# A mixture-of-experts block on one core: attention scores by column quarters of TensorE, turned by VectorE, and router logits by differences

## The chip, the core and the metric

The kernel runs on one core of a Trainium2 chip. TensorE (PE) multiplies 128x128 tiles, VectorE (DVE) and ScalarE (ACT) do elementwise work, GpSimd (POOL) does some of it too, and SyncE (SP) mostly issues transfers; each runs its own instructions in order and waits on semaphores. The metric is the device time of one execution in microseconds; before the change it is 472.56 us, the median of three runs (471.83 to 472.63).

## What is computed

All data are fp32. For 8 sequences of 512 tokens of width 256 (`x`), each with 64 context rows and an anchor vector:

```python
nx = layer_norm(x, gamma, beta)
scores = einsum('bth,bph->btp', nx @ Wq, ctx @ Wk) * 256 ** -0.5
weights = softmax(scores)
evidence = einsum('btp,bph->bth', weights, ctx @ Wv)
combined = concat([nx, evidence, anchor])                  # width 768
router_probs = softmax(combined @ router_W + router_b)     # 3 experts
h = silu(einsum('btc,ecr->bter', combined, e_w1) + e_b1)   # 3 x 512
routed = sum_e((h_e @ e_w2_e + e_b2_e) * router_probs_e)
g = sigmoid(silu(combined @ gate_w1 + gate_b1) @ gate_w2 + gate_b2)
out = x + g * (routed @ out_w + out_b)
```

Neither softmax changes when one number is taken from all the scores (or logits) of a token; the change rests on that.

## The kernel before

The eight sequences ("rows" b0, b1 of a pair) are worked in four pairs, j = 0 to 3. Most tensors are kept transposed, features on partitions and the 512 tokens of a sequence along the free dimension (`nxT`, `h`, `wT`). Products of a 2x2 block form, with the two sequences of a pair as one of the block indices, use seven products for eight (`nx_product` with numbers 1 to 7, sums of x from `combine_x`, sums of weights from `combine`).

**Setup.** Weights are loaded by SP; Wq and Wk are joined with the context into `mr` (`keep_m`), so that scores come straight from `nxT`. x of pair 0 is normalized (`statistics`, `deviation`, `normalize`) and transposed by TensorE (`transpose_x`), scores and softmax follow, then the weights `w` of pair 0 are transposed by four TensorE transposes (`transpose_w`, L583, called in `gate_layer` between products 5 and 2) and copied by ACT. Context values times first-layer weights are `vw` (`value_weights`). `anchor_rows` multiplies the anchors with 32 columns of the array at a time, into four quarters of the partitions.

**Scores** (`scores(b)`, L537): x is stationary (128 features x 128 tokens), `mr` moves, 64 context columns and 3 router columns, so tokens come out on partitions. 8 matmuls for a sequence, two of these calls for a pair. VectorE takes the maximum, ACT does four exps with sums. `router_logits(b)` multiplies the softmax weights with the three router rows of `vw` and sums, on VectorE, in two pieces, and adds the x part (from the score matmul) and the anchor's (`rbias`).

**A pair**: `gate_layer`, three `expert_layer`s, then `outputs`. The first three accumulate x parts and evidence parts (`evidence`, 64-row products) in PSUM; `keep_part` copies a bank by ACT, `add` adds one on VectorE; a product that goes on in a bank waits for the copy or addition that reads it. `weigh` multiplies hidden values by router probabilities on VectorE. `outputs` runs seven expert products per output block, and between them the next pair's scores, softmax, logits and probabilities.

**The order is written out by hand** and kept by the scheduler. Engines run their parts in program order. `put(within, (e, point), step)` places a step at a point of expert e (A after product 5 of the first chunk, B before products 7, C after them, D after products 3), "gate" before product 7 of the gate, "gate end" after its addition; `put(between, point, step)` at a point of `outputs`, whose order is begin, gate, P1, P5, P6, P2, P7, P3, P4. Buffers come from pools by tag: a tile with `bufs=1` reuses the buffer of the one before with that tag, and its writer waits until all readers of the old one are done. Transfers issued by SP or ACT share eight semaphores in program order: each waits until the eighth one before it has landed.

For pairs 1 to 3 the weights `w` go to DRAM and come back in 32x32 blocks (`regroup_w`, one store and four loads at P2), and VectorE turns the blocks (`transpose_w_blocks`). x of later pairs goes the same way (`store_x`, `regroup_x`, `transpose_blocks`).

Of the kernel before, what the change touches and what calls it, by code (L numbers as in the profile page):

```python
# [16 lines left out]
def kernel(  # L17
# [49 lines left out]

    nc = tc.nc
# [11 lines left out]
    SC = CT + E  # L80
# [41 lines left out]
    x_sb = {}  # L122

    def load_x(b):
        x_sb[b] = xpool.tile([P, NT, H], F32, tag="x", name=f"x_{b}")
        nc.sync.dma_start(x_sb[b], x[b].rearrange("(t p) d -> p t d", p=P))
# [24 lines left out]
    rrow = scr[:E, HK : HK + B]  # L151
# [3 lines left out]
    zeros, rows, cond_sb = scr[:, :P], scr[:, P : 2 * P], scr[:B, 2 * P : 2 * P + H]  # L155
    nc.vector.memset(zeros, 0.0)
# [19 lines left out]
    rw = const.tile([P, 3 * KH, E], F32, tag="rw", name="rw")  # L176
    nc.gpsimd.dma_start(rw, rows_of(router_W))
    rb_c = const.tile([E, 1], F32, tag="rb_c", name="rb_c")
    nc.gpsimd.dma_start(rb_c, router_b.rearrange("(e o) -> e o", o=1))
# [4 lines left out]
    w1 = const.tile([P, 2 * KH, R0 + E], F32, tag="w1", name="w1")  # L184
# [51 lines left out]

    mr = const.tile([P, KH, B, SC], F32, tag="mr", name="mr")
    nc.gpsimd.tensor_copy(w1[:, KH:, R0:], rw[:, KH : 2 * KH, :])
    for m in range(KH):
        nc.gpsimd.tensor_copy(mr[:, m, :, CT:], rw[:, m, :].unsqueeze(1).to_broadcast([P, B, E]))  # L240
# [15 lines left out]

    def small_transposes():
        pt = either("pt_rows")
        nc.tensor.transpose(pt[:, :NR], rows, ident[:NR, :NR])
        nc.vector.tensor_copy(cols, pt[:, :NR])  # L260
        nc.gpsimd.tensor_copy(b2T[:, :, :E], b2_c.rearrange("p e k -> p k e"))
        pt = either("pt_cond")
        for k in range(KH):
            nc.tensor.transpose(
                pt[:, k * B : (k + 1) * B], cond_sb[:, k * P : (k + 1) * P], ident[:B, :B]
            )
        nc.vector.tensor_copy(
            condT[:, :, :B], pt[:, : KH * B].rearrange("p (k b) -> p k b", b=B)
        )
# [48 lines left out]
    def keep_m(m, ps):  # L318
        nc.vector.tensor_copy(mr[:, m, :, :CT], ps.rearrange("p (b c) -> p b c", c=CT))
# [3 lines left out]
    rbias = const.tile([P, E, B], F32, tag="rbias", name="rbias")  # L323

    def router_anchor():
        ps = misc("ps_rb")
        for k in range(KH):
            nc.tensor.matmul(
                ps[:E, :B], rw[:, 2 * KH + k, :], condT[:, k, :B], start=(k == 0), stop=(k == KH - 1)
            )  # L330
        nc.vector.tensor_scalar(rrow, ps[:E, :B], rb_c, None, ALU.add)
        rbd = dram.tile([E, B], F32, tag="rbd", name="rbd")
        nc.gpsimd.dma_start(rbd, rrow)
        nc.gpsimd.dma_start(rbias, rbd.partition_broadcast(P))

    def spread_router_rows(j):
        vrd = dram.tile([E, 2 * CT], F32, tag="vrd", name=f"vrd_{j}")
        nc.gpsimd.dma_start(vrd.rearrange("e c -> c e"), S["vw", j][:, R0:])  # L338
        S["vr", j] = work.tile([P, E, 2, CT], F32, tag="vr", name=f"vr_{j}", bufs=1)
        nc.gpsimd.dma_start(  # L340
            S["vr", j].rearrange("p e i c -> p e (i c)"), vrd.partition_broadcast(P)
        )
# [40 lines left out]
    TB = 32  # L383
# [97 lines left out]
    def scale_x(b, k, src, vector):  # L481
        if vector:
            nc.vector.tensor_scalar(
                S["nxT", b][:, k, :], src, gamma_c[:, k : k + 1], beta_c[:, k : k + 1], ALU.mult, ALU.add
            )
        else:
            nc.scalar.activation(
                S["nxT", b][:, k, :], src, AF.Identity, bias=beta_c[:, k : k + 1],
                scale=gamma_c[:, k : k + 1],
            )  # L490

    def transpose_x(b):
        xn = S.pop(("xn", b))
        S["nxT", b] = npool.tile([P, KH, T], F32, tag="nxT", name=f"nxT_{b}")
        for k in range(KH):
# [3 lines left out]
            scale_x(b, k, pt, k % 2 == 0)  # L499

    def store_x(b):
        S["xd", b] = dram.tile([T, H], F32, tag="xd", name=f"xd_{b}")
        nc.sync.dma_start(S["xd", b].rearrange("(t p) d -> p t d", p=P), S.pop(("xn", b)))

    def regroup_x(b):
        xg = work.tile([P, KH, T], F32, tag="xg", name=f"xg_{b}", bufs=1)
        load_blocks(xg, S.pop(("xd", b)))
        S["xg", b] = xg

    def transpose_blocks(b):  # L510
# [3 lines left out]
        for k in range(KH):  # L514
            nc.vector.transpose(nxT[:, k, :], xg[:, k, :])
            scale_x(b, k, nxT[:, k, :], False)
# [12 lines left out]
    def scores(b):  # L529
        nxT, j, i = S["nxT", b], b // 2, b % 2  # L530
        if i == 0:
            S["w", j] = work.tile([P, NT, 2, CT], F32, tag="w", name=f"w_{j}", bufs=1)
        w = S["w", j][:, :, i, :]
        ps = misc(f"ps_s_{b}")[:, : NT * SC].rearrange("p (t c) -> p t c", c=SC)
        for t in range(NT):
            for k in range(KH):
                nc.tensor.matmul(  # L537
                    ps[:, t, :],
                    nxT[:, k, t * P : (t + 1) * P],
                    mr[:, k, b, :],  # L540
                    start=(k == 0),
                    stop=(k == KH - 1),
                )
        mx = work.tile([P, NT], F32, tag="mx", name=f"mx_{b}")
        nc.vector.tensor_reduce(mx, ps[:, :, :CT], AX.X, ALU.max)
        nmx = work.tile([P, NT], F32, tag="nmx", name=f"nmx_{b}")
        nc.vector.tensor_scalar_mul(nmx, mx, -SCALE)
        lg = work.tile([P, NT, E], F32, tag="lg", name=f"lg_{b}")
        nc.vector.tensor_copy(lg, ps[:, :, CT:])
        sm = work.tile([P, NT], F32, tag="sm", name=f"sm_{b}")  # L550
        for t in range(NT):
            nc.scalar.activation(
                w[:, t, :], ps[:, t, :CT], AF.Exp, bias=nmx[:, t : t + 1], scale=SCALE,
                accum_out=sm[:, t : t + 1],
            )
        S["lg", b], S["sm", b] = lg, sm

    def softmax(b):
        w, sm = S["w", b // 2][:, :, b % 2, :], S.pop(("sm", b))
        rs = work.tile([P, NT], F32, tag="rs", name=f"rs_{b}")  # L560
        nc.vector.reciprocal(rs, sm)
        nc.vector.tensor_tensor(w, w, rs.unsqueeze(2).to_broadcast([P, NT, CT]), ALU.mult)

    def regroup_w(j):

        wd = dram.tile([T, P], F32, tag="wd", name=f"wd_{j}")
        nc.sync.dma_start(
            wd.rearrange("(t p) c -> p t c", p=P), S["w", j].rearrange("p t i c -> p t (i c)")
        )
        S["wg", j] = work.tile([P, 1, T], F32, tag="wg", name=f"wg_{j}", bufs=1)  # L570
        load_blocks(S["wg", j], wd)

    def transpose_w_blocks(j):
        S["wT", j] = work.tile([P, T], F32, tag="wT", name=f"wT_{j}", bufs=1)
        nc.vector.transpose(S["wT", j], S.pop(("wg", j))[:, 0, :])

    def transpose_w(j):

        w = S["w", j]
        wT = work.tile([P, T], F32, tag="wT", name=f"wT_{j}", bufs=1)  # L580
        pt = misc(f"pt_w_{j}")
        for t in range(NT):
            nc.tensor.transpose(  # L583
                pt[:, t * P : (t + 1) * P], w[:, t, :, :].rearrange("p i c -> p (i c)"), ident
            )
        nc.scalar.copy(wT, pt)
        S["wT", j] = wT

    def router_logits(b):
        j, i = b // 2, b % 2  # L590
        w, lg, vr = S["w", j][:, :, i, :], S["lg", b], S["vr", j][:, :, i, :]
        le = work.tile([P, NT, E], F32, tag="le", name=f"le_{b}")
        pv = work.tile([P, NT // 2, E, CT], F32, tag="pv", name=f"pv_{b}", bufs=1)
        for t in range(0, NT, NT // 2):
# [653 lines left out]
```

## Time and profile before

| | |
|---|---|
| median of 3 runs | 472.56 us (471.83 to 472.63) |
| profiled execution | 472.56 us; its span from the first to the last instruction 470.4 us |
| PE busy | 465.1 us, 1439 instructions |
| DVE busy | 353.8 us, 653 instructions |
| ACT busy | 215.4 us, 388 instructions |
| POOL busy | 85.1 us, 111 instructions |
| granted TensorE clock, mean | 1.000 |
| score matmuls (L537) | 128 records, two for each fp32 matmul |

The profile's busy rows give an engine's busy time and its share of the span. Its slices cut the span into 40 equal parts, and each digit is the busy share in tenths (PEclk: the granted clock). The chain follows the work that ended last back through whatever released each step. Timeline rows have a start, a length, the engine, the line, the operation, output and inputs, the shape, and in brackets the engine's idle time before the row and who ended it. The rows of transfers give a size and the time from issue to landing. A pair's period, from the first gate product of one `outputs` to the next (`ps_gu`), is 107.55 us.

### The profile page before, as it was taken

To read this page: it belongs to the slowest core of one execution; us is meant where nothing else is said; L and a number is where in the kernel's file an instruction comes from. 1 tells how busy PE (TensorE), PEld (TensorE's weight loads), DVE (VectorE), ACT (ScalarE), POOL (GpSimd) and SP (SyncE) were. 2 spreads that over 40 slices of the span, in tenths; PEclk is the share of its full clock that TensorE was granted. 3 is DMA by queue.
4 is the path that set the end of the run, shared out by engine and by line. 5 is a ranking of instruction groups with operands and counts; after the bars stand their busy time and mean duration, and the time that the engine had idled before them with its cause. 6 is when DMAs were issued, how large, how long until landed. Compare 5 with 4: busy or idle time off the path is not lost.

```text
span 470.4 us, 4664 instructions
## 1 busy us (share of the span) xinstructions
PE 465.1 (99%) x1439; PEld 221.1 (47%) x1439; DVE 353.8 (75%) x653; ACT 215.4 (46%) x388; POOL 85.1 (18%) x111
## 2 busy tenths in 40 slices
PE   9999999999999999999999999999999999999996
PEld 7744546445444444445454444445454444444454
DVE  3755847989989555889989555898989624797972
ACT  3455565657211647657311546658311465457000
POOL 5318123200062300000062300000052400000020
PEclk9999999999999999999999999999999999999999
DMA  9968330056232830442122740352122560000013
GB/s 288 376 108 179 57 136 0 0 117 90 36 67 32 171 135 0 91 88 45 17 47 44 162 152 1 75 106 45 18 45 45 84 186 0 1 0 1 0 22 68
DMA packets 126424, 36.84 MB, mean 78 GB/s; under 512 B 111548, under 2 KB 123392, under 8 KB 125888
## 3 DMA queue, kind: packets, MB, share of 16 engines
q1 hardware_dynamic: 122656, 28.59, 29.1%
q0 software_dynamic: 1856, 7.18, 4.8%
q10 hardware_dynamic: 1888, 0.79, 0.6%
q8 instruction: 11, 0.18, 0.2%
q14 instruction: 13, 0.11, 0.1%
HBM read 28.36 MB, written 8.18 MB: 78 GB/s over the span
## 4 chain that ended last, share of the span: by engine, by line
PE 91%; DVE 4%; SPq 3%; DMA 0%; issue 0%; ACT 0%; ACTq 0%
PE ps_u L677 40%; PE ps_z L677 17%; PE ps_y L677 14%; PE ps_vw L652 4%; SPq L392 3%; PE ps_gu L677 3%; PE ps_s L537 3%; PE ps_w2o L418 2%; PE ps_gz L677 1%; DVE h L951 1%; PE ps_wake L255 1%; DVE h L760 1%; PE ps_m L299 1%; PE ps_v L299 1%; PE ps_gy L677 1%; DVE r L960 0%
## 5 line engine op out<-in xcount | busy, mean ns | idle before, releaser
L760 DVE TENSOR_TENSOR h<-h,pb 128x512 f32<-128x512 f32 x96 | 61.9, 693 | 10.5 <-ACT h L710 10.5
L677 PE MATMUL ps_u<-h,w2o 128*128 128x512 f32 x144 | 63.9, 593 | 0.0
L677 PE MATMUL ps_u<-nxT,w 128*128 128x512 f32 x112 | 55.6, 607 | 0.0
L710 ACT ACTIVATE h<-h,abias 128x512 f32<-128x512 f32 x72 | 49.2, 718 | 8.8 <-DVE h L716 8.2
L677 PE MATMUL ps_z<-wT,vw 64*128 64x512 f32 x104 | 49.5, 605 | 0.0
L983 POOL TENSOR_TENSOR yb<-yb,xb 128x512 f32<-128x512 f32 x14 | 19.1, 1368 | 150.1 <-DVE yb L982 144.7
L677 PE MATMUL ps_z<-h,w2s 128*128 128x512 f32 x96 | 42.8, 595 | 0.2 <-DVE r L966 0.2
L719 ACT COPY h<-ps_u 128x512 f32<-128x512 f32 x48 | 27.9, 582 | 32.2 <-PE ps_u L677 31.9
L677 PEld LDWEIGHTS ps_u<-h,w2o 128*128 128x128 f32 x144 | 27.1, 190 | 31.3 <-issue 29.4
L716 DVE TENSOR_TENSOR h<-h,ps_y 128x512 f32<-128x512 f32 x24 | 16.4, 683 | 28.9 <-PE ps_y L677 25.0
L951 DVE TENSOR_TENSOR h<-h,h 128x1024 f32<-128x1024 f32 x24 | 34.3, 1483 | 0.0
L677 PEld LDWEIGHTS ps_u<-nxT,w 128*128 128x128 f32 x112 | 19.9, 189 | 29.8 <-issue 24.9
L710 ACT ACTIVATE h<-ps_u,abias 128x512 f32<-128x512 f32 x24 | 16.5, 687 | 30.2 <-PE ps_z L677 30.2
L677 PE MATMUL ps_y<-nxT,w 128*128 128x512 f32 x56 | 28.6, 592 | 0.0
L677 PE MATMUL ps_z<-T,ws 128*128 128x512 f32 x56 | 28.6, 592 | 0.0
L677 PEld LDWEIGHTS ps_z<-h,w2s 128*128 128x128 f32 x96 | 17.9, 190 | 22.1 <-issue 21.1
L677 PE MATMUL ps_u<-wT,vw 64*128 64x512 f32 x56 | 27.8, 611 | 0.0
L338 POOL DMA_DIRECT2D vrd<-vw x4 | 3.2, 802 | 132.5 <-ACT vw L659 132.5
L677 PE MATMUL ps_y<-wT,vw 64*128 64x512 f32 x56 | 27.0, 596 | 0.0
L652 PE MATMUL ps_vw<-w,vT 128*128 128x512 f32 (+1 forms) x64 | 26.9, 541 | 0.0
L677 PE MATMUL ps_u<-T,ws 128*128 128x512 f32 x56 | 26.7, 594 | 0.0
L677 PE MATMUL ps_z<-nxT,ws 128*128 128x512 f32 x56 | 26.6, 592 | 0.0
(209 smaller groups left out, 790.2 us busy)
## 6 DMA issues: line engine op xcount, KB each, us to landing
pb<-pd POOLq DMA_DIRECT2D x4, 1536.0 KB, 7.7
x<-in_x_dram SPq DMA_DIRECT2D x8, 512.0 KB, 5.4
xb<-in_x_dram SPq DMA_DIRECT2D x64, 64.0 KB, 2.4
out_dram<-yb SPq DMA_DIRECT2D x56, 64.0 KB, 2.0
w<-in_L_xcond_e_w_dram SPq DMA_DIRECT2D x6, 512.0 KB, 9.5
xd<-x SPq DMA_DIRECT2D x6, 512.0 KB, 2.9
xg<-xd SPq DMA_DIRECT2D x48, 64.0 KB, 2.4
scr_wa<-in_L_xcond_e_w_dram SPq DMA_DIRECT2D x3, 512.0 KB, 10.2
```

The source lines that it names most:

```text
L299: nc.tensor.matmul(ps, w_sb[:, k, m * P : (m + 1) * P], src[:, k, :], start=(k == 0), stop=(k == KH - 1))
L392: nc.sync.dma_start(dst[i * TB : (i + 1) * TB, k, :].rearrange("r (j c) -> r j c", c=TB), src[:, lo : lo + TB].rearrange("(j r) c -> r j c ...
L418: nc.tensor.matmul(ps[:, d * H : (d + 1) * H], w2T[:, k, (i + d) * P : (i + d + 1) * P], ow_sb[:, k, :], start=(k == 0), stop=(k == KH - 1),)
L537: nc.tensor.matmul(ps[:, t, :], nxT[:, k, t * P : (t + 1) * P], mr[:, k, b, :], start=(k == 0), stop=(k == KH - 1),)
L652: nc.tensor.matmul(ps, vT[:, k, j * 2 * CT : (j + 1) * 2 * CT], w1[:, KH + k, n0:n1], start=(k == 0), stop=(k == KH - 1),)
L677: nc.tensor.matmul(ps, lhsT, rhs, start=start, stop=True, skip_group_check=not start)
L710: nc.scalar.activation(h, h if src is None else src, AF.Silu, bias=abias[:, c, 2 * j + i : 2 * j + i + 1])
L716: nc.vector.tensor_tensor(h, h, part, ALU.add)
L719: nc.scalar.copy(chunk(n, i, d), part)
L760: nc.vector.tensor_tensor(h, h, S["pb", j][:, i, 2 * q // RC, :], ALU.mult)
L951: nc.vector.tensor_tensor(d, p, m, ALU.subtract)
L983: nc.gpsimd.tensor_tensor(yb, yb, S["xb", 2 * j + row][:, i, :], ALU.add)
```

## The change

**Scores** are computed once for a pair. The context is stationary, 32 columns of it at a time; x moves, 256 tokens at a time. For row i and half h of the tokens the result goes to partitions 32(2i+h) and up, so four neighbouring matmuls use four column quarters. One VectorE transpose of 32x32 blocks brings tokens to partitions and context to the free dimension. A partition then holds one token of each of 8 blocks, so exps are eight for a pair, 128x64 each, as before.

**Router by differences.** Only logits 1 and 2 minus logit 0 are formed (ED = 2). Context row 0's column is taken from the other columns of `mr` (`keep_m`), so the score of context row 0 is 0 and its column is free: it carries difference 1's x part. Difference 2's x part is a VectorE multiply with a sum along x (`router_part`, four instructions of 128x256 for a sequence) against `gg`, gamma times the weight difference; the beta part goes into `rbias` by two more small matmuls. The context part uses two multiplies of 128x512 and two sums for a pair (`router_logits(j)`).

**Turning the weights** (`turn_weights`): VectorE transposes blocks into `tw`, and transfers from SBUF to SBUF move 32x256 pieces into `wT`: eight on SP's queue for later pairs, four on ACT's queue for pair 0 (there a second VectorE transpose writes the other four in place). This replaces the four TensorE transposes and the ACT copy of pair 0 and the way through DRAM of later pairs. `tw`, `junk` of `router_part` and `pv` of `router_logits` share one buffer (tag "tw").

**Layout.** `load_x` and `store_x` are four transfers of 32 partitions each instead of one of 128; `load_x` and `transpose_x` put the tokens in the order that the quarters need; the probabilities' buffer `pb` has a dimension for the half. SP issues 293 transfers (242 before), ACT 10 (6), POOL 52 (40).

**Places.** For pair 0, both `router_part` calls stand at "gate". A new point W lies between the fourth and fifth `weigh` of an expert. The rest is in the diff, cut to its core:

```diff
 def load_x(b):
-        nc.sync.dma_start(x_sb[b], x[b].rearrange("(t p) d -> p t d", p=P))
+        j, a = b // 2, b % 2
+        for i, h in SIDES:
+            nc.sync.dma_start(x_sb[b][side(i, h), :, :], tile_rows(x[2 * j + i], a, h))
...
 def keep_m(m, ps):
-        nc.vector.tensor_copy(mr[:, m, :, :CT], ps.rearrange("p (b c) -> p b c", c=CT))
+        ps = ps.rearrange("p (b c) -> p b c", c=CT)
+        nc.vector.tensor_copy(m0, ps[:, :, 0])
+        nc.vector.tensor_tensor(
+            mr[:, m, :, 1:], ps[:, :, 1:], m0.unsqueeze(2).to_broadcast([P, B, CT - 1]), ALU.subtract
+        )
...
+    def router_part(b):
+        j, a = b // 2, b % 2
+        lg = logits(j)
+        junk = work.tile([P, H], F32, tag="tw", name=f"junk_{b}", bufs=1)
+        for t in range(NT):
+            nc.vector.scalar_tensor_tensor(
+                junk, S["xn", b][:, t, :], 1.0, gg, ALU.mult, ALU.mult,
+                accum_out=lg[:, 2, a * NT + t : a * NT + t + 1],
+            )
...
+    def scores(j):
+        ps = misc(f"ps_s_{j}")
+        for g in range(2):
             for k in range(KH):
+                for i, h in SIDES:
+                    nc.tensor.matmul(
+                        ps[side(i, h), g * NH : (g + 1) * NH],
+                        mr[:, k, 2 * j + i, g * TB : (g + 1) * TB],
+                        S["nxT", 2 * j + i][:, k, h * NH : (h + 1) * NH],
+                        start=(k == 0),
+                        stop=(k == KH - 1),
+                    )
+        w = work.tile([P, 2, NJ, TB], F32, tag="w", name=f"w_{j}", bufs=1)
+        S["w", j] = w
+        nc.vector.transpose(w.rearrange("p g j c -> p (g j c)"), ps)
+        nc.vector.tensor_copy(logits(j)[:, 1, :], w[:, 0, :, 0])
+        nc.vector.memset(w[:, 0, :, 0], 0.0)
...
+    def turn_weights(j, queue, twice=False):
+        tw = work.tile([P, 2, NH], F32, tag="tw", name=f"tw_{j}", bufs=1)
+        nc.vector.transpose(
+            tw.rearrange("p g t -> p (g t)"), S["w", j].rearrange("p g j c -> p (g j c)")
+        )
         wT = work.tile([P, T], F32, tag="wT", name=f"wT_{j}", bufs=1)
...
+        if twice:
+            nc.vector.transpose(wT, S["w", j].rearrange("p g j c -> p (g j c)"))
+        for i, h in SIDES:
+            for g in range(2):
+                if not twice or g != h:
+                    queue.dma_start(wT[side(i, g), h * NH : (h + 1) * NH], tw[side(i, h), g, :])
...
+    def router_logits(j):
+        w, lg, vr = S["w", j], S["lg", j], S["vr", j]
+        le = work.tile([P, ED, NJ], F32, tag="le", name=f"le_{j}")
+        for e in range(ED):
+            pv = work.tile([P, 2, NJ, TB], F32, tag="tw", name=f"pv_{j}_{e}", bufs=1)
...
         if j == 0:
-            transpose_w(0)
+            turn_weights(0, nc.scalar, twice=True)
...
         if e > 1 or e and j:
-            weigh(j, 5)
+            weigh(j, 4)
+            run("W")
+            weigh(j, 1)
...
+                put(within, "gate", router_part, 0)
+                put(within, "gate", router_part, 1)
                 put(within, "gate", value_weights, 0, 1)
...
-                put(within, (0, "B"), router_logits, 1)
...
-                put(within, (0, "C") if j else (1, "A"), statistics, b1, 0, NT)
+                put(within, (0, "B") if j else (1, "A"), statistics, b1, 0, NT)
                 for i in range(2):
-                    put(within, (1, "C"), deviation, j + 1, i)
-                where = (1, "D") if j else (2, "B")
-                put(within, where, normalize, b0)
-                put(within, where, store_x, b0)
-                put(within, where, regroup_x, b0)
-                put(within, (2, "C"), normalize, b1)
-                put(within, (2, "C"), store_x, b1)
+                    put(within, (0, "D") if j else (1, "C"), deviation, j + 1, i)
+                for b, n in ((b0, (1, "W") if j else (1, "D")), (b1, (1, "A") if j else (2, "W"))):
+                    put(within, n, normalize, b)
+                    put(within, n, store_x, b)
+                put(within, (1, "C") if j else (2, "A"), regroup_x, b0)
+                put(within, (1, "B") if j else (2, "A"), router_part, b0)
+                put(within, (2, "W") if j else (2, "B"), router_part, b1)
...
-                put(between, "P1", scores, b0)
...
-                put(between, "P5", softmax, b0)
...
-                put(between, "P6", router_logits, b0)
-                put(between, "P2", scores, b1)
-                put(between, "P2", softmax, b1)
-                put(between, "P2", regroup_w, j + 1)
+                put(between, "P2", scores, j + 1)
...
+                put(between, "P7", softmax, j + 1)
...
-                put(between, "P7", router_logits, b1)
+                put(between, "P7", router_logits, j + 1)
+                put(between, "P7", turn_weights, j + 1, nc.sync)
...
-                put(between, "P3", transpose_w_blocks, j + 1)
...
```

## Prediction

> **What bounds the kernel now.** I read the busy rows, the slices, the chain, and then timelines of TensorE (PE) and VectorE (DVE) around every moved step.
>
> ```profile
> PE 465.1 (99%) x1439; PEld 221.1 (47%) x1439; DVE 353.8 (75%) x653; ACT 215.4 (46%) x388; POOL 85.1 (18%) x111
> ...
> PE   9999999999999999999999999999999999999996
> ...
> DVE  3755847989989555889989555898989624797972
> ...
> PEclk9999999999999999999999999999999999999999
> ...
> PE 91%; DVE 4%; SPq 3%; DMA 0%; issue 0%; ACT 0%; ACTq 0%
> ```
>
> PE has no gap to give: 99% busy at the full granted clock. A PE instruction saved is time saved, and any wait put in front of PE is time lost. DVE is at 8 and 9 tenths in slices 8 to 13 (82 to 153 us), the end of pair 0 and its outputs: DVE work added there has hardly an idle slot to lie in. All sums are against the profiled execution, 472.56 us (span 470.4), which is also the median.
>
> **1. The scores.** Before, each row of a pair has one burst of 16 records (8 fp32 matmuls, two records each) of 128x67. After, a pair has one burst of 16 matmuls, 32 records, with N=256 on 32 columns, four neighbours on the four column quarters. The nearest rows are the anchor rows (L356), which use such quarters now:
>
> ```profile
> 41.96 0.65 PE L356 MATMUL ps_ar<-scr_wa,condT 128*32 128x128 f32 x16
> 42.53 1.98 PE L677 MATMUL ps_u<-T,ws 128*128 128x512 f32 x4
> ```
> ```profile
> 111.37 1.90 PE L537 MATMUL ps_s<-mr,nxT 128*128 128x67 f32 x16
> 113.10 1.07 PE L677 MATMUL ps_z<-h,w2s 128*128 128x512 f32 x2
> ```
>
> Sixteen records with N=128 give way to the next matmul after 0.57 us: the trace has four starting 6 to 7 ns apart, then a step of about 109 ns. Four steps are 0.44, so going in and out costs some 0.13 here; by the starts just before and after, up to 0.33. The new burst is 32 records = 8 steps of about 0.215 (twice 0.109) = 1.72, plus 0.33 = 2.05 us. The old one is 113.10 - 111.37 = 1.73 per row, with the way in about 3.57 per pair. Gain 1.52 per pair, on PE's path in the outputs of pairs 0, 1 and 2: **-4.56 us**. Bound the other way: if quarters run one after another, 32 records of 0.216 (L418's 128x256: 16 in 3.45) are 6.9, a loss of 3.7 a pair with the way in.
>
> A rule speaks against this gain: the Trainium skill, "TensorE: Matmul & The Clock Gate", Part 3, says that weight loads overlap running matmuls only where the row group differs, which column quarters don't have, and gives 2.38 times for three column tiles. As an estimate from that page, four would give 3.2 times, 2.2 us and the way in and out, and a sum 1.4 us higher. The steps at L356 show no such load time, though each of its matmuls loads anew, and so I keep the row.
>
> **2. Setup to the first evidence product (pair 0).** Before:
>
> ```profile
> 33.70 0.42 DVE L666 TENSOR_TENSOR vw<-vw 64x256 f32<-64x256 f32 x1 [4.74 <-ACT vw L659]
> ...
> 36.73 0.69 DVE L716 TENSOR_TENSOR hg<-hg,ps_w 128x512 f32<-128x512 f32 x1 [0.45 <-PE ps_w L677]
> 41.27 0.69 DVE L716 TENSOR_TENSOR h<-h,ps_y 128x512 f32<-128x512 f32 x1 [3.85 <-DMA scr_w<-in_L_xcond_e_w_dram]
> ```
>
> (The bracket is DVE's idle time before the row.) The first evidence product starts at 33.84, the one into the gate's U bank at 35.66. Afterwards:
> - Scores need both rows' transposed x, so PE starts them at about 20.85 (19.79 before) and ends near 22.7. DVE's turn (0.69), the maximum and eight exps of 0.295 end at about 27.2; the Silu table (1.28) at 28.5.
> - DVE then has softmax, the copy of vw, both anchor transposes and combine_x before the two transposes of w, at about 31.1 to 31.8.
> - The four small DMAs that replace PE transposes go out on ACT's queue, 0.5 us each (31.85 to 33.85). Landing: small transfers take 2.4 us in a quiet stretch and 5.7 between 28 and 40 us,
>
> ```profile
> xb<-in_x_dram SPq DMA_DIRECT2D x64, 64.0 KB, 2.4
> ```
> ```profile
> scr_w<-in_L_xcond_e_w_dram SPq DMA_DIRECT2D x9, 64.0 KB, 5.7
> ```
>
>   I take 2.5, as these touch no DRAM: 36.4, so the first evidence product moves from 33.84 to 36.4. Ends: 2.0 and 6.5.
> - The scratch output of router_part shares its buffer (tag "tw") with the DMAs' source, so DVE can't begin the eight multiply-with-sums until the DMAs have landed. The trace has no such instruction of 128x256 with a sum. Nearest rows: the normalize's TENSOR_SCALAR of that size, four in 1.38 us (0.345 each); a 128x256 TENSOR_TENSOR alone, 0.42; and
>
> ```profile
> L960 DVE SCALAR_TENSOR_TENSOR r<-pb,b2o,r x16: 742/744/744, 112.1 to 435.0; 128x512 f32<-128x512 f32 x16
> ```
>
>   for twice the size. I take 0.46 (nearest to the 0.42 row, plus a little for handing out the sum); ends 0.345 and 0.65. Eight are 3.7: 40.1. Then the difference of vw (0.42) and the addition to U (0.69) that the U-bank product waits for: 41.2 in place of 35.66, **+5.6**.
>
> DVE's idle 4.74 before 33.70 doesn't cover it, for it lies before the landing; the four PE transposes of w that go (L583, 0.43) vanish in PE's wait. The two logit passes that leave expert 0 (3.2 us of DVE, one new pass of about 3.5 in their place) and a later PE let the one 0.36 us PE wait at 52.1 go (for the transposed second-layer weights): +5.3 net. Ends: 35.8 + 2.8 + 1.1 = 39.7, +3.7 net; 40.3 + 5.2 + 1.1 = 46.6, +10.5 net. The load of x in four DMAs puts six more issues (3 us) on SP ahead of the weights, twice; x of row 0 lands at 8.39 before, with 0.7 us to spare to its transposes, so 0 to +1. I take 0. In the later load the shift covers it.
>
> **3. Pair 0, expert 2.** The DVE and PE timelines before:
>
> ```profile
> 88.28 0.69 DVE L760 TENSOR_TENSOR h<-h,pb 128x512 f32<-128x512 f32 x1 [0.48 <-ACT h L710]
> ...
> 92.74 0.17 DVE L473 RECIPROCAL rstd<-sd 128x4 f32<-128x4 f32 x1
> 92.94 1.38 DVE L476 TENSOR_SCALAR x<-x,mv,rstd 128x256 f32<-128x256 f32 x4
> 94.24 1.28 DVE L716 TENSOR_TENSOR h<-h,ps_u 128x512 f32<-128x512 f32 x2
> ```
> ```profile
> 93.70 1.88 PE L677 MATMUL ps_z<-nxT,ws 128*128 128x512 f32 x4
> 95.42 1.88 PE L677 MATMUL ps_u<-T,w 128*128 128x512 f32 x4
> ```
>
> Product 4 (95.42) writes the U bank that the addition at 94.24 reads, and that addition is done at 94.9: slack 0.5 us. From 75 us DVE's only idle time here is that 0.48. The change puts ahead of the addition normalize of row b0 (at the end of expert 1) and b1 (new point W), 1.58 each; takes away b0's old place (1.58); adds two router_part, 8 x 0.46 = 3.7: +5.3 less the 0.48 = 4.8. Addition done at 99.75. On the way, the addition of Y(a), later by 2.6, holds a silu and behind it ACT's copy of U(b), 0.55 us on PE. PE: 99.75 less 95.42 = **+4.3** in all. Ends by 0.345 and 0.65 each: +3.4 and +5.8.
>
> **4. Pairs 1 and 2.** In expert 0 statistics of b1 (2.1 us, eight rows at 277.92 to 280.14 before) move ahead of the additions to U, done then at 279.4 against product 4 at 278.83: +0.6. In expert 2 one router_part stands before the addition of Y(a) and delays silu and the copy of U(b): about +0.5. Two pairs: **+2.2** (0 to 4).
>
> **5. The turned weights for the next pair.** Scores come once, at P2 (ending at about 236.4 for pair 1 to 2). Then DVE's turn behind the output's finish, the maximum, table load 1.28, eight exps: 243.0; softmax between output steps 249.3; logits 253.3; turn 254.0; eight SP issues of 0.53 and 2.2 to land: 260.4. The first evidence product is due at about 260.8. So just in time, with 0 to 1 us lost a pair: **+0.5** in all (0 to 3). DVE's logits get cheaper here (two 128x512 multiplies and sums for four of 128x384), ahead of this chain, and are in it. SP issues some 50 DMAs more (store_x in four, eight turns in place of five), POOL 12 more, at about 0.5 us each; outside the chain above PE waits for none of them, so I take 0 there.
>
> **Sum:** -4.56 + 5.3 + 4.3 + 2.2 + 0.5 = +7.7: **480.3 us**.
>
> **Rivals.**
> - *DVE has room* (faster). One mechanism: the additions to U are not what PE meets in steps 2 to 4, because DVE gets there first. Left are the gain -4.56, the later landing of wT (36.4 for 33.84, +2.56) and the lost 0.36 wait: **470.2**. For it: DVE idles 25% of the span, and 4.74 us just before 33.70. Against: slack at 95.42 is 0.5 us against 4.8 added. It decides if the queue ahead of the additions grows by under about a microsecond.
> - *Quarters one after another.* No gain but +3.7 in three pairs: 480.3 + 3 x 5.2 = **496**. Against it: the 6 to 7 ns starts at L356.
> - *The clock falls.* PE would stand still for some 3 us before the U-bank product and 3.8 us in expert 2. PEclk at 9 throughout shows no fall, since no stretch of the trace holds such a gap after 7 us. If PE then did half its work for 2 to 4 us in each place: +2 to +4, **484**. The skill's page "TensorE: Matmul & The Clock Gate", Part 1, says that an idle window of about 3.4 us halves the clock until as long a busy one; an estimate from that page: 1.7 us each, 483.7.
> - *Half the waits bite* (transfers land early and sums are cheap, the lost slots partly covered): about 472.6, no change.
>
> **Chances.** Forecast 0.58, DVE has room 0.20, no change 0.05, clock 0.12, serial quarters 0.05. A difference of about 0.2% (0.9 us) is what a measurement of this kernel can tell from none. Slower 0.75, same 0.05, faster 0.20. Range 469 to 487: the faster rival with a microsecond below, and up to the clock's 484 with the late landing's 3 us.
>
> **What would show it.** Scores: 32 records over about 1.72 us and the next matmul 2.05 after the first, in three outputs; 6.9 refutes it. First evidence product at 36.4, the U-bank product at 41 with DVE's idle time ended by the wT transfers; multiply-with-sum rows near 0.46. In expert 2 of pair 0 PE idle near 4 us, released by DVE's additions. Each of these stretches without PE idle time would make the forecast wrong by the term named. The period from one pair's first gate product (ps_gu) to the next, 107.55 us, should come out near 107.4 from pair 1 on.

## The result and the profile after

The changed kernel takes 501.41 us (median of six runs, 494.99 to 503.33); the kernel before, beside it, 472.48. The ratio is 1.0593, 95% interval 1.056 to 1.0627: slower, by 29 us where 8 were forecast. The profiled execution took 503.33 us with a span of 501.5, so the accounts below are against 31.1 us of span. It is the slowest of the six, so what is read from it below is held against the profiles of the later runs, which show much the same delays in setup and in pair 0, while the periods of pairs 1 and 2 differ from one execution to the next.

The page of the changed kernel, the lines that answer to those of before:

```profile
PE 473.0 (94%) x1439; PEld 213.6 (43%) x1439; DVE 361.6 (72%) x668; ACT 215.2 (43%) x385; POOL 96.9 (19%) x132
...
PE   8874999997999996999999998999999999999996
...
DVE  2854474797879935789888954988979925787972
...
PEclk9988799998999998999999999999999999999999
...
PE 59%; DVE 20%; DMA 12%; SPq 5%; issue 2%; ACT 1%; DVEq 0%
PE ps_u L774 30%; PE ps_z L774 11%; PE ps_y L774 9%; DMA x<-in_x_dram 5%; DMA ow_sb<-in_L_xcond_out_w_dram 4%; DVE h L1051 4%; PE ps_gu L774 3%; DVE h L858 3%; DVE junk L592 2%; PE ps_vw L749 2%; SPq L680 2%; SPq L1073 2%; PE ps_w2o L489 1%; PE ps_gz L774 1%; DMA w<-in_L_xcond_e_w_dram 1%
```

PE has holes now in the first tenth of the span and again at about 115 and 195 us, and the granted clock drops beside them. The chain runs through VectorE and through transfers: DMA and SP's queue hold 17% of it, against 3% before. PE's own busy time grew by 7.9 us with as many instructions, although the scores take less: that is work at half clock. The mean granted clock is 0.975 where it was 1.000, some 12 us over this span, part of them with PE idle anyway.

By the starts of the evidence product into the gate's U bank (first pair) and of each pair's first gate product, the 31.1 us divide so:

| stretch | before | after | difference | forecast |
|---|---|---|---|---|
| start to U-bank product | 35.66 | 50.80 | +15.1 | +5.6 (5.3 net) |
| from there to the outputs of pair 0 | 63.49 | 71.58 | +8.1 | +4.3 |
| period of pairs 0 to 1 | 107.55 | 114.05 | +6.5 | about -0.2 |
| 1 to 2 | 107.56 | 109.33 | +1.8 | about -0.2 |
| 2 to 3 | 107.55 | 106.04 | -1.5 | -1.5 |
| last pair's outputs | 48.62 | 49.74 | +1.1 | 0 |

**What worked.** The score burst in the outputs of pair 0, PE's timeline:

```profile
148.59 1.88 PE L774 MATMUL ps_y<-h,w2o 128*128 128x512 f32 x4
150.40 1.93 PE L635 MATMUL ps_s<-nxT,mr 128*32 128x256 f32 x32
152.26 1.98 PE L774 MATMUL ps_u<-h,w2o 128*128 128x512 f32 x4
```

All 32 records take 1.86 us to the next matmul, where two bursts of 1.73 stood. The quarters do run side by side, and the last period, in which nothing waits, is shorter by 1.51 us against 1.52 forecast.

**Setup.** PE's and ACT's rows that waited (in brackets how long and for whom), and the first and sixth multiply with sum on VectorE:

```profile
31.32 1.12 PE L774 MATMUL ps_z<-T,ws 128*128 128x512 f32 x2 [3.41 <-POOL ws L230]
...
39.79 1.12 PE L774 MATMUL ps_u<-nxT,w 128*128 128x512 f32 x2 [1.35 <-ACT hg L816]
42.64 1.15 PE L774 MATMUL ps_y<-wT,vw 64*128 64x512 f32 x1 [1.72 <-DMA wT<-tw]
...
50.80 1.22 PE L774 MATMUL ps_u<-wT,vw 64*128 64x512 f32 x1 [4.08 <-DVE hg L813]
```
```profile
34.86 4.25 ACTq L680 DMA_DIRECT2D wT<-tw  x4
39.15 0.59 ACT L816 COPY hg<-ps_u 128x512 f32<-128x512 f32 x1 [6.08 <-DMA ow_sb<-in_L_xcond_out_w_dram]
```
```profile
43.62 0.74 DVE L592 SCALAR_TENSOR_TENSOR junk<-x,gg 128x256 f32<-128x256 f32 x1 [8.79 <-DMA wT<-tw]
...
47.69 0.55 DVE L592 SCALAR_TENSOR_TENSOR junk<-x,gg 128x256 f32<-128x256 f32 x1
```

Two of the four waits were forecast (for wT and for the addition to U), but at 36.4 and 41.2 us and not at 42.64 and 50.80. Two were not: POOL's weight sums and ACT's copy. ACT's queue took 4.25 us for four issues, because the third and fourth waited for two weight loads that hold the same shared semaphores (`scr_wa` landed at 37.74, `ow_sb` at 38.57). The weights themselves were late, and the rate of the transfers shows why. The DMA view of 14 to 30 us in 40 slices, before and after:

```profile
DMA  9999999999999999999999999999999106906496
GB/s 394 379 384 399 384 369 399 394 379 384 394 394 364 394 399 374 374 405 389 374 389 394 379 410 346 361 366 341 255 208 105 25 24 104 38 0 98 69 43 21
```
```profile
DMA  9999999999999999999900096998439879998886
GB/s 366 394 384 389 379 404 374 374 404 384 379 389 399 374 389 389 351 389 410 205 0 0 0 15 26 36 46 61 87 113 195 215 231 282 302 277 225 200 184 123
```

Before, the queues move 380 KB per us until 25 us. After, everything stops at 21.7 and comes back over 5 us (some records of the stop may be missing, the landings are not: a 512 KB load lands at 20.03 and the next at 27.82). The change adds two kinds of transfer just ahead of that: 4-byte stores to DRAM on POOL's queue (`ggd`, issued at 16.29), and the router rows' stores, 2 us earlier than before.

### The profile page after: what moved, and what is told of

Same layout as the page of the kernel before. It is cut to its first block, busy times and chain, and to the rows that moved or that the text cites. A ratio compares the mean times of both kernels' runs of the same rounds, so it can differ in the third digit from the quotient of the medians.

```text
span 501.5 us, 4762 instructions
## 1 busy us (share of the span) xinstructions
PE 473.0 (94%) x1439; PEld 213.6 (43%) x1439; DVE 361.6 (72%) x668; ACT 215.2 (43%) x385; POOL 96.9 (19%) x132
## 4 chain that ended last, share of the span: by engine, by line
PE 59%; DVE 20%; DMA 12%; SPq 5%; issue 2%; ACT 1%; DVEq 0%
PE ps_u L774 30%; PE ps_z L774 11%; PE ps_y L774 9%; DMA x<-in_x_dram 5%; DMA ow_sb<-in_L_xcond_out_w_dram 4%; DVE h L1051 4%; PE ps_gu L774 3%; DVE h L858 3%; DVE junk L592 2%; PE ps_vw L749 2%; SPq L680 2%; SPq L1073 2%; PE ps_w2o L489 1%; PE ps_gz L774 1%; DMA w<-in_L_xcond_e_w_dram 1%
## 5 line engine op out<-in xcount | busy, mean ns | idle before, releaser
L807 ACT ACTIVATE h<-h,abias 128x512 f32<-128x512 f32 x72 | 49.3, 719 | 31.2 <-DVE h L813 31.1
L774 PE MATMUL ps_u<-nxT,w 128*128 128x512 f32 x112 | 57.4, 619 | 2.2 <-ACT hg L816 1.4
L774 PE MATMUL ps_z<-wT,vw 64*128 64x512 f32 x104 | 53.1, 642 | 0.0
L774 PE MATMUL ps_u<-T,w 128*128 128x512 f32 x56 | 29.9, 655 | 9.5 <-DVE h L813 9.5
L403 POOL DMA_DIRECT2D vrd<-vw x8 | 5.0, 629 | 157.5 <-ACT vw L756 157.5
L774 PE MATMUL ps_u<-wT,vw 64*128 64x512 f32 x56 | 30.4, 659 | 4.1 <-DVE hg L813 4.1
L774 PE MATMUL ps_y<-wT,vw 64*128 64x512 f32 x56 | 29.6, 645 | 1.7 <-DMA wT<-tw 1.7
L813 DVE TENSOR_TENSOR h<-h,ps_z 128x512 f32<-128x512 f32 x24 | 16.1, 686 | 17.1 <-PE ps_z L774 17.1
```

The costliest lines, as they stand in the source:

```text
L774: nc.tensor.matmul(ps, lhsT, rhs, start=start, stop=True, skip_group_check=not start)
L807: nc.scalar.activation(h, h if src is None else src, AF.Silu, bias=abias[:, c, 2 * j + i : 2 * j + i + 1])
L813: nc.vector.tensor_tensor(h, h, part, ALU.add)
```

## The experiments

All start from the changed kernel unless the kernel before is named. My theory A after the result: waits in setup, and the late x of pairs 1 and 2, come from the order of queues. B: transfers stall, by the 4-byte store (B1) or by the router rows' stores (B2).

**e1, x in one transfer.**

```diff
-        for i, h in SIDES:
-            nc.sync.dma_start(x_sb[b][side(i, h), :, :], tile_rows(x[2 * j + i], a, h))
+        nc.sync.dma_start(x_sb[b], x[b].rearrange("(t p) d -> p t d", p=P))
```

> The changed kernel with x loaded by one transfer for a sequence, as before (in the old token order, so the tokens go to other places than the rest of the kernel takes them to be). Theory A, the four-part loads are what hurts: in setup they keep the weights back and hold the shared transfer semaphores that the w pieces wait for; in pairs 1 and 2 the last parts fall behind the 1.5 MB probabilities transfer and the statistics wait. Then setup gets 3 to 6 us shorter, PE's waits of 4.1 and 2.5 us before product 4 of expert 0 go with the clock's loss behind them (8 us in all): 487 to 490 us. Rival B, transfers are slow from 21.7 us on because of the 4-byte router rows and sums that POOL writes to DRAM: setup stays as it is, and the time is about 493.

492.2 us, ratio 1.0417 (1.0401 to 1.0432). The periods fall to 107.64 and 107.40: in pairs 1 and 2 A is right. Setup does not change (U-bank product 51.33), though x and the first weights come sooner: the stop in the transfers comes 1.2 us sooner too, as `ggd` is issued 1.2 us sooner. That spoke for B.

**e2, weight sums first on POOL; e3, router_part out of the gate; e4, statistics back at C.**

```diff
+        combine_weights(E)
         store_router_rows(0)
         spread_router_bias()
-        combine_weights(E)
```
```diff
-                put(within, "gate", router_part, 0)
-                put(within, "gate", router_part, 1)
+                put(within, (0, "A"), router_part, 0)
+                put(within, (0, "A"), router_part, 1)
...
-        junk = work.tile([P, H], F32, tag="tw", name=f"junk_{b}", bufs=1)
+        junk = work.tile([P, H], F32, tag="junk", name=f"junk_{b}", bufs=1)
```
```diff
-                put(within, (0, "B") if j else (1, "A"), statistics, b1, 0, NT)
+                put(within, (0, "C") if j else (1, "A"), statistics, b1, 0, NT)
```

> The changed kernel with the gate's weight sums (combine_weights) ahead of the router rows' and bias transfers on POOL, as before. Theory A, POOL waits in order: the sums end near 23 us in place of 33.5, and PE's 3.4 us wait before product 5 goes; but the w pieces still land at 42 to 43 us, so the U-bank product stays near 50 and the time changes by less than 1 us: 500 to 501. Rival, the later PE is what makes all that follows late: 496 to 498.

> The changed kernel with pair 0's two router_part calls moved from the gate to point A of expert 0, with a buffer of their own. Theory A, they stand before the addition to U and cost their 5.8 us there, while VectorE has 5.6 us idle in expert 0: the U-bank product comes at about 45.5 in place of 50.8, and the time falls by 4 to 6 us: 495 to 497. Rival, VectorE is late anyway (the weights arrive late): they cost the same further on, and the time stays within 1 us of 501.

> The changed kernel with the second row's statistics for pairs 1 and 2 back at point C of expert 0, behind the additions to U. Theory A: PE's waits of 4.1 and 2.5 us before product 4 and about 2 us of half clock behind the first go: 492 to 493. Rival, the first row's statistics, which also wait for x (5.2 us of VectorE idle in pair 1), hold the additions as long: less than 2 us gained, 499 to 501.

e2: 499.35 (ratio 1.0573, 1.0556 to 1.0591). The U-bank product stays late (51.33), as A had it; what differs lies in the first two periods (108.55 and 110.54), which differ between executions anyway. e3: 498.34 (1.0513, 1.0451 to 1.0576); the U-bank product comes at 49.24, 1.6 us sooner and not 5, because ACT's four issues take 6.92 us there (4.25 in the changed kernel) with the same shared semaphores: the last piece lands at 44.63 in place of 43.32, ACT's copy behind the issues is late, and the first evidence product starts 3 us later. Its eight multiplies, with POOL idle beside them, take 0.42 us each and 0.46 from one to the next. Its executions spread from 493 to 501 us: inconclusive on its own. e4: 494.88 (1.0461, 1.0439 to 1.0483); the periods fall to 107.21 and 106.67, below the 107.4 of the forecast. A is right there, its rival wrong; e8 and e9, which share the edit, have 106.9 to 107.4.

**e5, gg by matmul, and e6, the store alone in the kernel before.** In e5 two matmuls of a broadcast column with the identity spread gg, and both the store and the load of gg go; in e6 the kernel before gets the store and nothing else:

```diff
+        for k in range(KH):
+            nc.tensor.matmul(
+                pg[:, k * P : (k + 1) * P], ggc[:, k : k + 1].to_broadcast([P, P]), ident,
+                start=True, stop=True,
+            )
+        nc.scalar.copy(gg, pg[:, :H])
...
-        nc.gpsimd.dma_start(ggd.rearrange("o (k p) -> p (o k)", p=P), ggc)
```
```diff
         nc.gpsimd.tensor_copy(b2T[:, :, :E], b2_c.rearrange("p e k -> p k e"))
+        nc.gpsimd.dma_start(ggd.rearrange("o (k p) -> p (o k)", p=P), gamma_c)
```

> The changed kernel with the row gg (gamma times router weights) spread over the partitions by two small matmuls and a copy in place of a 4-byte-wise store to DRAM (ggd) and a load. In the runs so far every transfer stalls about 5.4 us after that store is issued, and the weights land 8 us late. Theory B1, that store is the cause: the weights of expert 1 land near 22 us in place of 27.8, the w pieces by about 38, the U-bank product near 46 in place of 50.8, and the time falls by 4 to 7 us: 494 to 497. Rival B2, the two stores of router rows (vrd), issued earlier than before, are the cause: the stall stays at about 21.7 us, and the time within 2 us of 501.

> The kernel before with one transfer more: the same store of a 128x2 tile to DRAM in 4-byte pieces on POOL's queue at the same place (nothing reads it). Theory B1: transfers stall from about 5.4 us after its issue, near 19 to 21 us, the weights land some 5 us later, PE waits for them in setup, and the time rises by 2 to 6 us: 475 to 478. Rival B2: no stall there, 472.5 to 473.

e5: 494.4 us (1.0474, 1.0458 to 1.049), 7.0 less. The stop at 21.7 is gone (from 28 us the rate falls to 25 KB per us, as it does before); the U-bank product came only to 49.50, because the matmuls stood in a place where PE waited for POOL and then ran at half clock: the scores start at 25.20 there and at 21.86 in the changed kernel. So e5 does not say what the store costs in setup; most of its gain lies behind it. e6 is the clean one: 478.39 us (1.0139, 1.0121 to 1.0157). **One store of 1 KB costs the kernel before 6 us.** Its DMA view, 14 to 30 us, and POOL's timeline:

```profile
DMA  9999999999999990019928845999776996499999
GB/s 389 389 384 389 384 379 389 394 389 379 389 356 384 410 256 0 15 31 41 97 92 133 113 102 123 138 159 189 261 277 266 225 179 102 82 307 369 412 351 356
```
```profile
14.31 0.76 POOL L264 DMA_DIRECT2D ggd<-cols  x1 [0.31 <-issue]
15.95 0.66 POOL L336 DMA_DIRECT2D rbd<-scr_k  x1 [0.88 <-DVE rstd L476]
26.29 0.60 POOL L337 DMA_DIRECT2D rbias<-rbd  x1 [9.68 <-DMA rbd<-scr_k]
```

The rate falls to nothing 5.4 us after the issue, as in the changed kernel, and POOL waits 9.68 us for the next small store (4.5 before). PE pays later, behind a U-bank product that is hardly late (35.89), with a 3.44 us wait for the late second-layer weights and half clock after it. Before, and in e6:

```profile
52.91 3.88 PE L418 MATMUL ps_w2o<-ow_sb,scr_w2T 128*128 128x256 f32 x16 [0.20 <-DVE scr_w2T L410]
```
```profile
56.98 5.35 PE L421 MATMUL ps_w2o<-ow_sb,scr_w2T 128*128 128x256 f32 x15 [3.44 <-DVE scr_w2T L413]
```

B1 is shown: the store alone makes the stop.

**e7, no router_part in pair 0's expert 2** (the x part of pair 1's third logit is left out).

```diff
-                put(within, (1, "B") if j else (2, "A"), router_part, b0)
-                put(within, (2, "W") if j else (2, "B"), router_part, b1)
+                if j:
+                    put(within, (1, "B"), router_part, b0)
+                    put(within, (2, "W"), router_part, b1)
...
-            nc.gpsimd.memset(S["lg", j][:, 0, :], 0.0)
+            nc.gpsimd.memset(S["lg", j], 0.0)
```

> The changed kernel without the two router_part calls in expert 2 of pair 0 (pair 1's third logit lacks its x part). Theory A: there they put the additions to U 8 x 0.63 = 5 us behind, so that PE's 3.4 us wait, the 0.6 us one before it and 1.7 us of half clock go: from the U-bank product to the first gate product of the outputs 66 us in place of 71.6, and the time falls by 5 to 6: 495 to 496. Rival, the waits come from normalize, which stands in new places: 1 to 2 us less.

502.09 us (1.0633, 1.0583 to 1.0683): no gain in all, by my own edit. The wider memset made VectorE's first write to `lg` wait 12.7 us for POOL, which stood behind a transfer; the U-bank product came at 58.21. The stretch that the run was for went from 71.58 to 65.41 us, 6.2 less: theory A there.

**e8, e9, e10, undone together.** e8 is e5 with e2's and e4's edits. e9 is gg by matmul after the anchor rows, with e2's, e3's and e4's edits. e10 is e9 with

```diff
+                put(within if j else between, (1, "B") if j else "P1", router_part, b0)
+                put(within if j else between, (2, "W") if j else "P5", router_part, b1)
```

> Three undone parts together: gg by matmul, the gate's weight sums first on POOL, and the second row's statistics at C in pairs 1 and 2. Theory B1 with A: U-bank product near 44 (the 3.4 us wait for the sums goes too), periods of pairs 1 to 3 near 107, 106.7 and 106.04: 501.4 - 7 - 8 = 485 to 488. With B2 only the statistics' 7 us and some of POOL's are gained: 491 to 493.

> Five undone parts: gg by two matmuls after the anchor rows (no 4-byte store), the gate's weight sums first on POOL, the second row's statistics at C in pairs 1 and 2, and pair 0's router_part at A of expert 0 with its own buffer. If these are the causes in setup, the w pieces land at 36 to 38 us, the U-bank product comes at 39 to 41 (35.7 before), the rest of pair 0 keeps its +6 to 8, the periods are near 107, 107, 106: 477 to 481. If the way of the w pieces (VectorE's queue, two turns, four transfers) is late for a reason of its own, the U-bank product stays above 44: 484 or more.

> As the run before, and pair 0's two router_part calls of expert 2 moved into the outputs (P1 and P5). PE's wait of 3.4 us and the half clock behind it in expert 2 go: 5 to 6 us less than the run before. If VectorE is full there too (8 to 9 tenths), the w pieces of pair 1 land some 3 us late and PE waits for them at the next gate: only 2 to 3 us less.

e8: 491.83 (1.0415, 1.0399 to 1.043), more than forecast, with the matmuls' bad place still in it (U-bank product 50.19). e9: 484.56 (1.0247, 1.0227 to 1.0267): U-bank product at 43.21, so 7.6 of setup's 15.1 us are undone, by these edits together. e10: 481.53 (1.019, 1.0175 to 1.0205): the stretch to the outputs falls from 70.22 to 65.08, and 1.7 us come back in the next period (107.38 to 109.07). That is the size of its second case, but not its wait: PE waits 1.74 us in the outputs for VectorE's combination, which the moved multiplies stand in front of, and not for the w pieces. PE in expert 2 of e10:

```profile
102.10 1.13 PE L781 MATMUL ps_u<-nxT,w 128*128 128x512 f32 x2 [0.48 <-ACT h L823]
103.06 1.88 PE L781 MATMUL ps_z<-nxT,ws 128*128 128x512 f32 x4
104.78 1.93 PE L781 MATMUL ps_u<-T,w 128*128 128x512 f32 x4
```

Only half a microsecond of wait is left where the changed kernel waits 3.28 (shown below).

**e11, x in pieces of 128 partitions x 256; e12, e10 with x in one transfer** (as in e1).

```diff
+        src = x[2 * j : 2 * j + 2].rearrange("i (h a t r) d -> (i h) r a t d", h=2, a=2, r=TB)
+        for t in range(NT):
+            nc.sync.dma_start(x_sb[b][:, t, :], src[:, :, a, t, :])
```

> As the run before, and x loaded in four pieces of 128 partitions x 256 instead of 32 partitions x 1024 (as many transfers). Theory: pieces on 32 partitions move slowly (about 210 KB per us from 7 to 11 us against 340 with one transfer for a sequence); then this one moves 320 or more there, x is there 1 to 2 us earlier, PE's half us waits at 13 to 16 us go: 1 to 2 us less than the run before. Rival, the number of transfers sets the rate: no difference.

> The version with six parts undone or moved (gg by matmul, weight sums first, statistics at C, both pairs' router_part moved, own buffer), and x by one transfer for a sequence (tokens in the old order, so they go to other places than the rest takes them to be). If the slow x pieces are what still makes the scores of setup start near 23.5 us in place of 19.8, they start near 20.5, the U-bank product comes at 40 to 41 in place of 43.5, and the time is 477.5 to 479. If not, it stays at 481.5.

e11: 497.95 (1.0536, 1.0512 to 1.0559), 16 us worse than e10; both cases wrong. From 7 to 11 us the transfers move 94 KB per us on average with the engines busy a quarter of the time, against some 210 in e10 and 340 with one transfer in e1. The shape of a piece sets the rate, and of the three this is the worst. e12: 477.82 (1.0107, 1.0086 to 1.0127): scores start at 20.83, the U-bank product at 40.63 (43.47 in e10). The pieces of x cost 3.7 us, 2.8 of them in setup.

**e13, e14, what about the store stalls the rest.** The kernel before with e6's store as 128 pieces of 8 bytes (`"o (p k) -> p (o k)"`), and with e6's store on SP's queue (`nc.sync.dma_start`).

> The kernel before with the added store as 128 pieces of 8 bytes in place of 256 of 4 (the same 1 KB, the same queue and place). If the number of small pieces sets the stall, it is about half: 474.5 to 476. If any store of small pieces stalls all transfers alike: 478. If only 4-byte pieces do it: 472.5.

> The kernel before with the added store of 4-byte pieces on SP's queue in place of POOL's. If the writes themselves stall the transfers, the time is about 478 again, or more, since SP's weight loads wait behind it. If it is POOL's queue that makes them slow: 472.5 to 474.

e13: 473.12 (1.0014, 1.0 to 1.0028). e14: 474.3 (1.0044, 1.0031 to 1.0058). So 256 pieces of 4 bytes on POOL's queue cost 6 us, half as many of twice the size at most 1.3, and 4-byte pieces on SP's queue 2. The times alone would lay it on POOL's queue, near e14's second case, but the transfers say otherwise. Their rates from 14 to 30 us in 40 slices, e13 and then e14, and PE's wait for the second-layer weights in e14:

```profile
GB/s 405 389 369 389 399 384 374 399 389 384 380 381 394 374 236 159 189 261 282 328 246 230 277 220 256 297 251 430 371 358 364 376 289 249 148 101 37 27 112 18
```
```profile
GB/s 389 384 394 384 379 394 384 389 384 394 379 389 389 389 379 385 394 319 360 410 343 102 82 26 23 44 72 74 103 116 171 167 192 194 192 214 237 228 177 161
```
```profile
53.86 3.88 PE L421 MATMUL ps_w2o<-ow_sb,scr_w2T 128*128 128x256 f32 x16 [1.24 <-DVE scr_w2T L413]
```

In e14 the store is issued at 13.79 and the rate falls to 23 KB per us from 22.4 on, nearly as deep and as long as in e6, 2.7 us later. So the stop comes with SP's queue too, and with half as many pieces of twice the size it is only a dip, to 159. What the queue changes is when the stop comes and what it costs: PE waits 1.24 us for the second-layer weights in e14 and 3.44 in e6. Number and size of the pieces were changed together and are not told apart. The Trainium skill, "DMA: Bandwidth & Descriptors", Specifications, says that pieces under 512 bytes miss the full rate, through a read and a write back. That fits the direction of e13; no run here shows the read and write back, and that entry gives no reason for other loads to stop. Why they stop stays open.

No version of the changed kernel beats the kernel before. The best that computes the whole function is e10, 1.9% slower.

## Why the prediction was wrong

Its direction was right and its mechanisms in PE and VectorE were; it failed on transfers, which it had put at nothing in three places: the load of x in pieces, the added transfers on SP and POOL, and the statistics' wait for x.

1. *Scores, -1.52 a pair.* Right: -1.51. The weight loads don't show, as the row had it and against the page weighed there: 32 records in 1.86 us. Old and new way in were both taken some 0.1 us too long, which cancels.
2. *Setup, +5.3 net.* Measured +15.1. The step that failed is "0 to +1. I take 0" for the load of x, and with it "outside the chain above PE waits for none of them, so I take 0 there" for the added transfers of SP and POOL. The x pieces cost 3.7 us (e10 to e12). The store `ggd`, one of those transfers, costs 6.3 in the kernel before (e6), nearly all of it behind the U-bank product, and 7.0 here (e5), of which the profiles place only 1.3 in setup, where e5's scores start 3.3 us late. The prediction set the landing of the w pieces at 36.4 with an end at 40.3; they landed at 42.3 to 43.3, since ACT's issues waited for weight loads on the shared semaphores and the two turns ended at 34.8 and not 31.8. Of the 9.6 us between 41.2 and 50.80, 7.2 are this landing and 2.2 the slower multiplies of point 3. How the 7.2 divide between the x pieces, `ggd` and POOL's new order was not measured; e9 undoes the last two and the multiplies' place, e12 the first as well. That e12's U-bank product, at 40.63, comes near 41.2 is chance: the forecast's 41.2 holds 3.7 us of multiplies that e12 has moved away, and the pieces land at 38.4 there. So no run shows the forecast's way of w by itself.
3. *The eight multiplies with sums, 0.46 each.* In expert 2 exactly that (0.42 and a 0.08 read of the sum, one each 0.46). In the gate 0.73 on average, because POOL worked beside them: 0.78 to 0.87 apart while POOL's rows are 128x256, 0.59 while they are 128x128. Where POOL stood idle (e3, expert 2 here) each took 0.42.
4. *Pair 0, expert 2, +4.3.* Right in mechanism, a little small. VectorE's and PE's rows after:

```profile
112.08 0.42 DVE L592 SCALAR_TENSOR_TENSOR junk<-x,gg 128x256 f32<-128x256 f32 x1
112.43 0.08 DVE L592 DVE_READ_ACCUMULATOR junk<-x,gg 128x1 f32 x1
...
116.17 1.28 DVE L813 TENSOR_TENSOR h<-h,ps_u 128x512 f32<-128x512 f32 x2
```
```profile
112.18 1.45 PE L774 MATMUL ps_z<-nxT,ws 128*128 128x512 f32 x3
116.91 2.96 PE L774 MATMUL ps_u<-T,w 128*128 128x512 f32 x4 [3.28 <-DVE h L813]
```

   3.28 us for the additions, 0.5 for the copy of U(b) before, and after it the clock rival's term: the four matmuls and the first evidence products lose about 1.7 us at half clock. The other 2.6 of the stretch's 8.1 us belong mostly to setup, as the half clock after its last wait (2.4 in the 4.8 us of point 7). Taking the two calls away gives 5.2 (e9 to e10) to 6.2 (e7).
5. *Pairs 1 and 2, +2.2.* Measured 11.3 against the last period. The forecast counted the 2.1 us of statistics, and not that they wait for x. The rows of pair 1, by queue:

```profile
180.78 4.04 SPq L143 DMA_DIRECT2D x<-in_x_dram  x8
```
```profile
177.85 2.02 POOL L729 DMA_DIRECT2D pd<-prT  x4 [1.51 <-DVE prT L726]
182.46 0.57 POOL L733 DMA_DIRECT2D pb<-pd  x1 [2.58 <-DMA pd<-prT]
```
```profile
190.32 0.43 DVE L535 BATCH_NORM_STATS2 st<-x 128x6 f32<-128x256 f32 x1 [5.16 <-DMA x<-in_x_dram]
```
```profile
191.93 1.88 PE L774 MATMUL ps_z<-nxT,ws 128*128 128x512 f32 x4
197.71 2.93 PE L774 MATMUL ps_u<-T,w 128*128 128x512 f32 x3 [3.89 <-DVE h L813]
```

   Eight issues of x take 4.04 us (two took 1.15 before), and the 1.5 MB of probabilities are issued in the midst of them, where before they came 6 us after the last x issue:

```profile
156.17 1.15 SPq L126 DMA_DIRECT2D x<-in_x_dram  x2
```

   The first three parts land 2.6 to 2.7 us after their issue, the other five after 7.8 to 9.0. Both ways of undoing it (e1: fewer issues; e4: nobody waits) bring the periods back. How many parts fall behind differs between executions (five of pair 1's eight here, three in e2 and in e3), which is why e2 and e3, that touch nothing there, show other periods (108.5 and 110.5 to 111).
6. *The turned weights in time, +0.5.* About right: no wait of PE for wT in pairs 1 to 3; the last piece lands at 176.94.
7. *Rivals.* The clock was given 0.12 and happens, beside the forecast and not in place of it. By windows of the changed kernel's setup (the clock is the last but two):

```profile
42.60:46.60 4.00, 3.96 (x8) 1.63 (x8) 2.88 (x7) 0.00 (x0) 3.92 (x7) 0.57 0.40 63
46.60:50.80 4.20, 0.12 (x2) 0.00 (x1) 4.00 (x13) 0.00 (x0) 3.06 (x5) 0.85 0.46 144
50.80:55.60 4.80, 4.80 (x10) 1.75 (x11) 1.83 (x3) 0.72 (x1) 0.00 (x0) 0.50 0.82 170
```

   After PE's 4.08 us wait come 4.8 us at half speed. In this profile waits of 3.28 us and more were followed by such a stretch, and the 2.36 us wait in pair 2 was not. The estimate of 1.7 us for one place is what expert 2 shows. That an idle time of about 3.4 us is needed, as the page cited for it has it, does not hold here: in e2 and e3 the wait at the same place in pair 2 took 1.92 and 2.40 us, and half clock followed.

The last pair's 1.1 us was not followed up; it is 0.3 to 0.7 in e9 to e12. What remains of setup in e12, 5 us, holds the way of w (turn, four transfers) and a wait of e12's own, 3.83 us of PE ahead of the matmuls that spread gg with half clock behind it; it was not taken apart further.

## What to carry to other kernels

Price every transfer that a change adds, also those that nobody waits for: a 1 KB store in 4-byte pieces cost 6 us because other loads stopped, and splitting a load changed its rate from 340 to 210 or 90 KB per us. Before moving a step up that reads a loaded tile, look up when that tile lands, and which large transfer is issued next to it. When PE is the bound and every wait of some 3.3 us costs half as much again in clock, as it did here, a gain of 1.5 us a pair is lost by one such wait.

## What the runs showed of the hardware

- A DRAM store of 256 pieces of 4 bytes stopped the other transfers: on POOL's queue 5.4 us after its issue, in every run that had it there, from 380 KB per us to under 40, and back over 5 us or more; on SP's queue 8.6 us after its issue (e14). With 128 pieces of 8 bytes the rate only dipped, to 159 (e13).
- Of three ways to load the same 512 KB, while x loads the queues move 340 KB per us with one transfer, 210 with four of 32 partitions x 4 KB, 90 with four of 128 partitions x 1 KB.
- A multiply with a sum of 128x256 on VectorE took 0.46 us with the read of its sum, and 0.59 to 0.87 from one to the next while POOL was computing.
- Sixteen matmuls of 32 columns and N=256 on four column quarters took 1.86 us.
